# A Mamba block's state scan merged over four channel groups, its input product issued ahead of the product with C, its head in twelve steps, and growing chunks

## The chip, the cores and the metric

The kernel runs on one core of one Trainium2 chip. The metric is the device time of one execution in microseconds (us). The kernel before takes 4009.58 us (median of three runs, 4000.31 to 4012.51). Every run told here was of the fast state, and every kernel's result agreed with the reference. The engines are called PE (TensorE), DVE (VectorE), ACT (ScalarE) and POOL (GpSimd). The account below takes it that each works through its own instructions in the order in which they stand in its queue. The traces agree with that where an engine stands idle in front of one instruction with others behind it; no run tests it. A hole is idle time of an engine between two of its instructions, DVE's where no other is named.

## The reference, cut to what matters

The network has four layers over 3327 nodes. The change lies in layer 1, which runs a graph convolution and puts its normalised output through a Mamba block:

```python
xconv = sum((xpad[k:k + L] * conv_w[:, k] for k in range(D_CONV))) + conv_b
u = jax.nn.silu(xconv)
dbc = u @ w_xp
dt = jax.nn.softplus(dbc[:, :DT_RANK] @ w_dt + b_dt)
B = dbc[:, DT_RANK:DT_RANK + D_STATE]
C = dbc[:, DT_RANK + D_STATE:]
A = -jnp.exp(A_log)
dA = jnp.exp(dt[:, :, None] * A[None])
dBu = dt[:, :, None] * B[:, None, :] * u[:, :, None]

def step(hst, inp):
    dAt, dBut, Ct = inp
    hst = dAt * hst + dBut
    return (hst, hst @ Ct)
_, ys = lax.scan(step, jnp.zeros((D_INNER, D_STATE), h.dtype), (dA, dBu, C))
y = ys + u * D_skip
y = y * jax.nn.silu(z)
return y @ w_out
```

There are 512 inner channels (four groups of 128 partitions) and 16 states. The nodes, padded to 3328, are the sequence. The recurrence runs along it, so channels lie on partitions and nodes on the free axis, in chunks of up to 512.

## The kernel before

For each chunk and each of the 16 states, the kernel does this (cut; `w` is the chunk's width, `NG` is 4, `DS` is 16):

```python
def rows(x, s):                       # issued one state ahead
    parts, dt, du = x
    pb = psum.tile([P, WC], F32, name="ps")[:, :w]
    nc.tensor.matmul(pb, three[:, s:s + 1].to_broadcast([3 * BC, P]), parts, ...)   # B on all partitions
    B = work.tile([P, 1, WC], F32, name="row", bufs=2)[:, :, :w]
    nc.scalar.copy(B[:, 0, :], pb)                                                  # "the row"
    dA = work.tile([P, NG, WC], F32, name="dA")[:, :, :w]                           # two buffers
    for g in range(NG):
        nc.scalar.activation(dA[:, g, :], dt[:, g, :], AF.Exp, scale=A[:, g, s:s + 1])
    return B, dA

def scan(x, s, B, dA):
    C = cpsum.tile([P, 1, WC], F32, name="C")[:, :, :w]
    nc.tensor.matmul(C[:, 0, :], three[:, DS + s:DS + s + 1].to_broadcast([3 * BC, P]), parts, ...)
    db = [...]                                                                      # input product, two halves
    for i in range(2):
        nc.vector.tensor_mul(db[i], du[:, 2 * i:2 * i + 2, :], B.to_broadcast([P, 2, w]))
    h = work.tile([P, NG, WC], F32, name="h")[:, :, :w]
    for g in range(NG):                                                             # four scans
        nc.vector.tensor_tensor_scan(h[:, g, :], dA[:, g, :], db[g // 2][:, g % 2, :],
                                     initial=carry[:, s, g:g + 1], op0=ALU.mult, op1=ALU.add)
    nc.scalar.copy(carry[:, s, :], h[:, :, w - 1])
    nc.vector.tensor_mul(h, h, C.to_broadcast([P, NG, w]))                          # product with C
    return h
```

The row and C are made by PE in PSUM, the memory that PE writes its results to; few PSUM buffers are shared by all these steps. `carry` keeps the last value of each scan, with which the next chunk starts. After each product with C, four matmuls with the identity add `h` to the sums over states (`y` in the profile). Between these stands other work on the same queues. `pump()` does a step of the graph convolution (four matmuls at a time, then its norm and transposes; `rs` in the profile is the norm's factor, a power that GpSimd makes). The states 2 to 5 project the gate. The states 7 to 15 run the head of the next chunk in steps, which makes its `u`, `parts`, `dt` and `du`. `back()` writes out the chunk that ended. The head's costliest step for ACT and PE is this one, called the dt step below:

```python
for g in range(NG):
    ps = psum.tile([P, WC], F32, name="ps")           # two buffers, shared with the row's matmul
    nc.tensor.matmul(ps[:, :w], w_dt[3 * BC:, g * P:(g + 1) * P], left[3 * BC:], ...)
    nc.scalar.activation(v[:, g, :], ps[:, :w], AF.Identity, bias=b_dt[:, g:g + 1])
    nc.scalar.activation(e[:, g, :], ps[:, :w], AF.Abs, bias=b_dt[:, g:g + 1])
```

Of the kernel before, what the change touches and what calls it, by code (L numbers as in the profile page):

```python
# [9 lines left out]
F32 = mybir.dt.float32  # L10
BF16 = mybir.dt.bfloat16
I32 = mybir.dt.int32
AF = mybir.ActivationFunctionType
# [29 lines left out]
def gnn_kernel(ctx: ExitStack, tc: tile.TileContext, n: int, a: dict, out: bass.AP):  # L43
# [88 lines left out]
    with tc.tile_pool(name="l1b", bufs=1) as wpool, tc.tile_pool(name="l1at", bufs=2) as l1at:  # L132
# [29 lines left out]
        with tc.tile_pool(name="l1aw", bufs=1) as cwork, tc.tile_pool(name="l1c", bufs=2) as ch, \  # L162
# [50 lines left out]
            nch = -(-npad // WC)  # L213
            ends = [npad - c * WC for c in range(nch)][::-1]
# [8 lines left out]
            def convolve():  # L223

                rest = None
                for it in range(nt):
                    cb = cpsum.tile([P, 2, D], F32, name="cb")
                    acc, tp = cb[:, 0, :], cb[:, 1, :]
                    for j in range(nt):
# [5 lines left out]
                        if j % JC == JC - 1:  # L235
                            if rest is not None:
                                rest()
                                rest = None
                            yield it
                    m = cwork.tile([P, D], F32, name="m")  # L240
                    nc.scalar.copy(m, acc)
                    yield it
# [9 lines left out]
                    mv = small.tile([P, 2], F32, name="mv")  # L252
                    stats(mv, h)
                    rs = small.tile([P, 1], F32, name="rs")
                    power(rs, mv[:, 1:2])
                    standardize(h, h, mv[:, 0:1], rs)

                    def rest(it=it, h=h):
# [9 lines left out]
                    yield it  # L268
                rest()
                yield nt  # L270
# [42 lines left out]
            def head(c):  # L313
# [7 lines left out]
                nc.vector.tensor_copy(xc[:, :, :3], last)  # L321
                u = us[c] = ch.tile([P, NG, WC], F32, name="u")[:, :, :w]
                for g in range(NG):
                    nc.scalar.copy(xc[:, g, 3:3 + w], project(c, g, w))
                    ug = u[:, g, :]
                    nc.scalar.activation(ug, xc[:, g, 0:w], AF.Identity, scale=conv_w[:, g, 0:1],
                                         bias=conv_b[:, g:g + 1])
                    for k in range(1, 4):
                        nc.vector.scalar_tensor_tensor(ug, xc[:, g, k:k + w], conv_w[:, g, k:k + 1], ug,
                                                       op0=ALU.mult, op1=ALU.add)  # L330
                    yield None
                nc.vector.tensor_copy(last, xc[:, :, w:w + 3])
                nc.scalar.activation(u, u, AF.Silu)
                yield None
# [7 lines left out]
                nc.scalar.copy(left, ps[:3 * BC + DTR, :w])  # L342
                nc.vector.tensor_sub(left[:3 * BC], left[:3 * BC], parts)
                for k in (1, 2):
                    nc.scalar.copy(parts[k * BC:(k + 1) * BC], left[k * BC:(k + 1) * BC])
                nc.vector.tensor_sub(parts[2 * BC:], left[2 * BC:3 * BC], parts[2 * BC:])
# [3 lines left out]
                v, e, e1 = (scratch()[:, :, :w] for _ in range(3))  # L350
# [6 lines left out]
                yield None  # L357
                nc.scalar.activation(e, e, AF.Exp, scale=-1.0)
                nc.scalar.activation(e1, e, AF.Identity, bias=1.0)
                nc.vector.scalar_tensor_tensor(e, e1, 1.0, e, op0=ALU.subtract, op1=ALU.subtract)  # L360
                nc.scalar.activation(e1, e1, AF.Ln)
# [8 lines left out]
                yield parts, dt, du  # L370

            def gate_input(c, g):
                w = us[c].shape[2]
                if g == 0:
                    szs[c] = ch.tile([P, NG, WC], F32, name="sz", bufs=1)[:, :, :w]
                nc.scalar.activation(szs[c][:, g, :], project(c, NG + g, w), AF.Silu)

            def rows(x, s):

                parts, dt, du = x  # L380
# [5 lines left out]
                dA = work.tile([P, NG, WC], F32, name="dA")[:, :, :w]  # L386
                for g in range(NG):
                    nc.scalar.activation(dA[:, g, :], dt[:, g, :], AF.Exp, scale=A[:, g, s:s + 1])  # L388
                return B, dA

            def scan(x, s, B, dA):

                parts, dt, du = x
                w = dt.shape[2]
# [3 lines left out]
                db = [work.tile([P, 2, WC], F32, name="db", bufs=3)[:, :, :w] for _ in range(2)]  # L398
                for i in range(2):
                    nc.vector.tensor_mul(db[i], du[:, 2 * i:2 * i + 2, :], B.to_broadcast([P, 2, w]))  # L400
                h = work.tile([P, NG, WC], F32, name="h")[:, :, :w]
                for g in range(NG):
                    nc.vector.tensor_tensor_scan(h[:, g, :], dA[:, g, :], db[g // 2][:, g % 2, :],  # L403
                                                 initial=carry[:, s, g:g + 1], op0=ALU.mult, op1=ALU.add)
                nc.scalar.copy(carry[:, s, :], h[:, :, w - 1])
                nc.vector.tensor_mul(h, h, C.to_broadcast([P, NG, w]))  # L406
                return h

            def gate(c, ys):
                u = us[c]  # L410
                w = u.shape[2]
                for g in range(NG):
                    nc.vector.tensor_mul(u[:, g, :], ys[g][:, :w], szs[c][:, g, :])

            def back(c):

                u = us[c]
                m = u.shape[2] // P
# [20 lines left out]
            for x in head(0):  # L439
                pump()  # L440
# [730 lines left out]
```

## Time and profile before

| kernel before | us |
|---|---|
| span of the profiled run | 4006.0 |
| first scan starts | 450.3 |
| node 768 done (third 512 chunk opens) | 763.0 |
| last product with C ends | 1677.9 |
| layer 2 entered (its first result) | 1707.7 |
| rest of the program | 2298.3 |

The prediction below shows the views that this was read from. One is added here: the waits of DVE in a single steady chunk (1142 to 1333 us), because the block's totals hide where the time lies. The columns are the engine, what waited, what it waited for, the us in total, the number of waits and the longest.

```profile
DVE h L406 <- PE C L396: 4.9, 2, 3.0
DVE m L87 <- POOL rs L221: 3.7, 4, 1.6
...
DVE db L400 <- ACT row L385: 1.9, 2, 1.0
```

A chunk of 191 us thus has only 15 us of holes, from many releasers. The row of B costs hardly 2 of them.

### The profile page before, as it was taken

To read this page: it belongs to the slowest core of one execution; us is meant where nothing else is said; L and a number is where in the kernel's file an instruction comes from. 1 tells how busy PE (TensorE), PEld (TensorE's weight loads), DVE (VectorE), ACT (ScalarE), POOL (GpSimd) and SP (SyncE) were. 2 spreads that over 40 slices of the span, in tenths; PEclk is the share of its full clock that TensorE was granted. 3 is DMA by queue.
4 is the path that set the end of the run, shared out by engine and by line. 5 is a ranking of instruction groups with operands and counts; after the bars stand their busy time and mean duration, and the time that the engine had idled before them with its cause. 6 is when DMAs were issued, how large, how long until landed. Compare 5 with 4: busy or idle time off the path is not lost.

```text
span 4006.0 us, 41676 instructions
## 1 busy us (share of the span) xinstructions
PE 3596.0 (90%) x15071; PEld 2625.0 (66%) x15071; DVE 2724.7 (68%) x6003; ACT 1675.1 (42%) x2690; POOL 367.1 (9%) x436
## 2 busy tenths in 40 slices
PE   8999988888888877689999999999999899999985
PEld 7888754444444433378877777777777677777764
DVE  1111589999999989867743443443452999999996
ACT  0000555455554555211112333333344666666662
POOL 0000000101010101011110000000000122222210
PEclk9999999999999988889999999999999999999997
DMA  6442211111111000044422111121102122122100
GB/s 218 138 143 92 76 50 40 35 40 35 35 35 37 20 0 0 15 146 142 142 83 75 56 59 49 52 60 57 46 24 86 58 62 62 53 61 61 54 22 7
DMA packets 98960, 252.96 MB, mean 63 GB/s; under 512 B 13858, under 2 KB 48034, under 8 KB 98610
## 3 DMA queue, kind: packets, MB, share of 16 engines
q1 hardware_dynamic: 98738, 250.14, 20.0%
q8 instruction: 122, 2.00, 0.2%
q14 instruction: 100, 0.82, 0.1%
HBM read 239.88 MB, written 10.22 MB: 62 GB/s over the span
## 4 chain that ended last, share of the span: by engine, by line
PE 34%; DVE 16%; ACT 3%; issue 2%; POOL 2%; DMA 0%; POOLq 0%; ACTq 0%; DVEq 0%
PE acc L751 11%; PE acc L719 7%; PE acc L649 6%; PE sc L707 3%; DVE cand L759 3%; DVE e L892 2%; DVE e L893 2%; PE tp L747 2%; PE pj L917 1%; DVE z L829 1%; DVE top L768 1%; DVE z L873 1%; DVE rest L770 1%; ACT junk L827 1%; ACT junk L848 1%
## 5 line engine op out<-in xcount | busy, mean ns | idle before, releaser
L403 DVE TENSOR_TENSOR_SCAN h<-dA,carry,db 128x512 f32<-128x512 f32 (+1 forms) x448 | 510.7, 1191 | 0.1
L459 PE MATMUL y<-h,ident 128*128 128x512 f32 (+1 forms) x896 | 436.1, 633 | 76.7 <-DVE h L406 76.6
L759 DVE MAX8 cand<-e 128x8 f32<-128x128 f32 x676 | 143.8, 280 | 494.6 <-ACT e L708 494.6
L751 PE MATMUL acc<-G,wt 128*128 128x256 f32 x1352 | 342.9, 408 | 48.4 <-ACT wt L749 48.4
L459 PEld LDWEIGHTS y<-h,ident 128*128 128x128 f32 x896 | 185.9, 215 | 290.8 <-issue 175.9
L749 ACT COPY wt<-tp 128x512 f32<-128x512 f32 (+1 forms) x364 | 185.9, 552 | 438.3 <-PE tp L747 438.2
L751 PEld LDWEIGHTS acc<-G,wt 128*128 128x128 f32 x1352 | 268.9, 204 | 120.7 <-ACT wt L749 82.2
L234 PE MATMUL cb<-F,at 128*128 128x256 f32 x1352 | 334.2, 393 | 9.3 <-ACT m L251 9.2
L708 ACT COPY e<-sc 128x416 f32<-128x416 f32 (+1 forms) x416 | 192.5, 508 | 327.8 <-PE sc L707 327.8
L751 PE MATMUL acc<-X,wt 128*128 128x256 f32 x1352 | 326.0, 386 | 3.0 <-ACT wt L749 2.8
L719 PE MATMUL acc<-X,at 128*128 128x256 f32 x1352 | 320.8, 387 | 2.7 <-POOL e L701 2.7
L234 PEld LDWEIGHTS cb<-F,at 128*128 128x128 f32 x1352 | 261.1, 196 | 90.9 <-issue 33.5
L649 PE MATMUL acc<-F,at 128*128 128x257 f32 x1352 | 311.2, 384 | 2.5 <-DVE at L646 2.5
L719 PE MATMUL acc<-F,at 128*128 128x256 f32 x1352 | 308.8, 380 | 0.0
L113 PE MATMUL acc<-xa,at 128*128 128x257 f32 x1352 | 308.3, 381 | 0.0
L719 PEld LDWEIGHTS acc<-X,at 128*128 128x128 f32 x1352 | 250.8, 191 | 76.1 <-issue 41.8
L751 PEld LDWEIGHTS acc<-X,wt 128*128 128x128 f32 x1352 | 250.3, 191 | 63.8 <-ACT wt L749 33.5
L388 ACT ACTIVATE dA<-dt,A_log 128x512 f32<-128x512 f32 (+1 forms) x448 | 280.9, 681 | 12.6 <-DVE dt L365 12.2
L707 PE MATMUL sc<-kT,q 64*128 64x416 f32 x832 | 259.8, 561 | 26.0 <-ACT e L708 26.0
L113 PEld LDWEIGHTS acc<-xa,at 128*128 128x128 f32 x1352 | 255.7, 191 | 37.5 <-issue 0.7
L719 PEld LDWEIGHTS acc<-F,at 128*128 128x128 f32 x1352 | 249.5, 189 | 46.5 <-issue 13.7
L649 PEld LDWEIGHTS acc<-F,at 128*128 128x128 f32 x1352 | 254.1, 192 | 37.4 <-DVE at L646 2.7
(297 smaller groups left out, 5358.7 us busy)
## 6 DMA issues: line engine op xcount, KB each, us to landing
at<-in_adjT SPq DMA_DIRECT2D x104, 832.0 KB, 4.4
at<-in_adjT SPq DMA_DIRECT2D x156, 448.0 KB, 3.3
at<-in_adjT SPq DMA_DIRECT2D x52, 576.0 KB, 3.7
at<-in_adjT SPq DMA_DIRECT2D x52, 320.0 KB, 2.9
at<-in_adjT SPq DMA_DIRECT2D x26, 512.0 KB, 3.5
xa<-in_x SPq DMA_DIRECT2D x1, 3328.0 KB, 13.5
xt<-in_xT SPq DMA_DIRECT2D x26, 128.0 KB, 4.0
qd<-q SPq DMA_DIRECT2D x52, 64.0 KB, 1.5
```

What stands on the lines that cost most here:

```text
L113: nc.tensor.matmul(acc, at[:, j, :], rhs[:, j0 + j, :], start=(j0 + j == 0), stop=(j0 + j == nt - 1))
L234: nc.tensor.matmul(acc, at[:, j % JC, :], X0[:, j, :], start=(j == 0), stop=(j == nt - 1))
L388: nc.scalar.activation(dA[:, g, :], dt[:, g, :], AF.Exp, scale=A[:, g, s:s + 1])
L403: nc.vector.tensor_tensor_scan(h[:, g, :], dA[:, g, :], db[g // 2][:, g % 2, :], initial=carry[:, s, g:g + 1], op0=ALU.mult, op1=ALU.add)
L459: nc.tensor.matmul(ys[g][:, :w], ident, h[:, g, :], start=False, stop=(s == DS - 1))
L649: nc.tensor.matmul(acc, at[:, j, :], F[:, j0 + j, :], start=(j0 + j == 0), stop=(j0 + j == nt - 1))
L707: nc.tensor.matmul(pl[:, :w], q[h:h + DA, :], kT[p][h:h + DA, c0:c0 + w], start=True, stop=True)
L708: nc.scalar.copy(e[:, c:c + w], pl[:, :w])
L719: nc.tensor.matmul(acc, at[:, j, :], rhs[:, j0 + j, :], start=(j0 + j == 0), stop=(j0 + j == nt - 1))
L749: nc.scalar.copy(wt[:, :m, :], pt[:, :m, :])
L751: nc.tensor.matmul(acc, wt[:, j, :], rhs[:, j0 + j, :], start=(j0 + j == 0), stop=(j0 + j == nt - 1))
L759: nc.vector.max(cand[:, s * 8:(s + 1) * 8], z[:, s * SEG:(s + 1) * SEG])
```

## The change

The change means to take instructions and waits off DVE, the full engine, and to start it earlier. It puts a column in front of each group, with decay 0 and the carried state as input, so that one scan runs over all four groups. It issues the next state's input product ahead of the product with C. It moves the carry copies and some small steps to GpSimd, and standardizing to ACT. It spreads the head of the next chunk over twelve states, and it lets the chunks grow: 128, 256, 384, then 512. The core of the diff (the split of the convolution's steps and of the end of a chunk is cut):

```diff
-            nch = -(-npad // WC)
-            ends = [npad - c * WC for c in range(nch)][::-1]
+            ends = []
+            while not ends or ends[-1] < npad:
+                prev = ends[-1] if ends else 0
+                ends.append(min(npad, prev + min(WC, (len(ends) + 1) * P)))
+            nch = len(ends)
...
-                    standardize(h, h, mv[:, 0:1], rs)
+                        nb = small.tile([P, 1], F32, name="nb")
+                        nc.gpsimd.tensor_scalar(nb, mv[:, 0:1], rs, -1.0, op0=ALU.mult, op1=ALU.mult)
+                        nc.scalar.activation(h, h, AF.Identity, scale=rs, bias=nb)
...
-                nc.scalar.activation(szs[c][:, g, :], project(c, NG + g, w), AF.Silu)
+                nc.scalar.copy(szs[c][:, g, :], project(c, NG + g, w))
...
-                dA = work.tile([P, NG, WC], F32, name="dA")[:, :, :w]
+                dA, db = (by_group(x[s % 2], w) for x in (dAs, dbs))
+                if s < 2 and (c == 0 or w != ends[c - 1] - starts[c - 1]):
+                    nc.gpsimd.memset(dA[:, :, 0:1], 0.0)
+                nc.gpsimd.tensor_copy(db[:, :, 0], carry[:, s, :])
...
-                for g in range(NG):
-                    nc.vector.tensor_tensor_scan(h[:, g, :], dA[:, g, :], db[g // 2][:, g % 2, :],
-                                                 initial=carry[:, s, g:g + 1], op0=ALU.mult, op1=ALU.add)
-                nc.scalar.copy(carry[:, s, :], h[:, :, w - 1])
-                nc.vector.tensor_mul(h, h, C.to_broadcast([P, NG, w]))
+                nc.vector.tensor_tensor_scan(h[:, :m], dAs[s % 2][:, :m], dbs[s % 2][:, :m],
+                                             initial=0.0, op0=ALU.mult, op1=ALU.add)
+                nc.gpsimd.tensor_copy(carry[:, s, :], h[:, :, w])
...
+                    if nxt:
+                        B = rows(*nxt)
+                    h = scan(x, s)
+                    if s == 0 and c:
+                        gate(c - 1, ys)
+                    if nxt:
+                        feed(*nxt, B)
+                    nc.vector.tensor_mul(h, h, C.to_broadcast([P, NG, w]))
+                    if nxt:
+                        C = reader(*nxt)
...
-                    if s >= DS - 9 and c + 1 < nch:
+                    if s == 8:
+                        nc.scalar.activation(szs[c], szs[c], AF.Silu)
+                    if DS - 13 <= s < DS - 1 and c + 1 < nch:
```

## The prediction

> **What bounds the kernel now.** I read the busy tenths of the page first, to find the stage that the change touches, then busy time by stretch, then the waits of the vector engine (DVE), then the groups by shape, then the order in time.
>
> The page, the span in 40 slices of 100 us:
>
> ```profile
> PE   8999988888888877689999999999999899999985
> DVE  1111589999999989867743443443452999999996
> ACT  0000555455554555211112333333344666666662
> ```
>
> The Mamba block is the stretch from slice 4 to slice 16: DVE stands at 9 while ACT stands at 5 and TensorE (PE) at 8, and TensorE's busy time has modelled ends, so it is less full than it looks. The graph convolution of the same layer runs inside this stretch on TensorE, and its work there ends near 1397 us.
>
> The stretches are the chunks of the sequence; their borders I took from the products du<-dt,u that open each chunk (441, 575, 763, 954, 1142, 1333, 1520 us) and the last gate (1680 us). After the length come busy us with instruction counts, granted clock, DMA share, GB/s:
>
> ```profile
> core 0: us, PE busy (x) PEld busy (x) DVE busy (x) ACT busy (x) POOL busy (x), PEclk, DMA share, GB/s
> 442.00:575.00 133.00, 118.55 (x511) 88.01 (x510) 101.28 (x146) 81.19 (x166) 3.80 (x8) 1.00 0.21 64
> 575.00:763.00 188.00, 159.19 (x471) 88.30 (x472) 172.04 (x155) 98.30 (x162) 10.87 (x12) 0.93 0.12 37
> 763.00:954.00 191.00, 164.97 (x497) 93.00 (x496) 175.44 (x161) 97.27 (x161) 16.73 (x14) 0.93 0.12 36
> ...
> 1333.00:1520.00 187.00, 143.15 (x371) 70.04 (x370) 173.20 (x155) 103.27 (x188) 13.41 (x10) 0.87 0.01 3
> 1520.00:1680.00 160.00, 115.47 (x287) 55.37 (x286) 155.69 (x129) 75.76 (x158) 11.20 (x6) 0.87 0.00 0
> ```
>
> A chunk of 512 lasts 187 to 191 us, of which DVE works 172 to 176: it is the bound, with about 15 us of holes per chunk. The first chunk (256 wide) is different: 133 us for 101 us of DVE work, with no engine full; it is ruled by handovers. Over 450 to 1690 us DVE is busy 1133 of 1240 us. The view of its waits says what the 107 us of holes are:
>
> ```profile
> DVE h L406 <- PE C L396: 26.2, 13, 3.1
> DVE db L400 <- ACT row L385: 24.9, 16, 6.8
> DVE m L87 <- POOL rs L221: 21.7, 21, 4.0
> ```
>
> The groups by shape, for the cost of one instruction (mean ns after the comma):
>
> ```profile
> L403 DVE TENSOR_TENSOR_SCAN h<-dA,carry,db 128x512 f32<-128x512 f32 x384 | 467.4, 1267 | 0.1
> L400 DVE TENSOR_TENSOR db<-du,row 128x1024 f32<-128x1024 f32 x192 | 229.9, 1213 | 15.1 <-ACT row L385 14.9
> L406 DVE TENSOR_TENSOR h<-h,C 128x2048 f32<-128x2048 f32 x96 | 218.8, 2280 | 23.1 <-PE C L396 20.7 <-ACT carry L405 2.4
> L403 DVE TENSOR_TENSOR_SCAN h<-dA,carry,db 128x256 f32<-128x256 f32 x64 | 43.2, 732 | 0.0
> ```
>
> These means overstate what an instruction occupies, because neighbours overlap. The order in time shows it:
>
> ```profile
> 1658.07 2.28 DVE L406 TENSOR_TENSOR h<-h,C 128x2048 f32<-128x2048 f32 x1
> 1660.27 1.22 DVE L400 TENSOR_TENSOR db<-du,row 128x1024 f32<-128x1024 f32 x1
> 1661.41 4.80 DVE L403 TENSOR_TENSOR_SCAN h<-dA,carry,db 128x512 f32<-128x512 f32 x4
> 1666.13 1.20 DVE L400 TENSOR_TENSOR db<-du,row 128x1024 f32<-128x1024 f32 x1
> 1667.25 2.28 DVE L406 TENSOR_TENSOR h<-h,C 128x2048 f32<-128x2048 f32 x1
> ```
>
> From start to start, four scans take 4.72 us (1.18 each, not 1.267), a half input product 1.12 and the product with C 2.20. One state takes 9.17 us. It also shows that the order on the engine is not the program's: half of the next state's input product already stands between the scans and the product with C.
>
> **What the Trainium skill says.** "VectorE: DVE Perf Modes", section on the TRN2 errata: a fixed extra latency per instruction, so few large tiles are cheaper than many small ones. The trace agrees but makes it small: from 256 to 512 elements the scan's start-to-start time goes from 0.65 us (four in 2.67 us, the last one 0.73) to 1.18, that is 2.08 ns per element and about 0.11 us fixed. "SBUF — State Buffer", section Who interferes with whom: a DVE instruction with two SBUF inputs blocks a GpSimd instruction that reads SBUF until it finishes. The trace agrees: the 128x1 addition on GpSimd at 826.36 took 1.10 us beside a scan that ran 826.19 to 827.44, where alone (379.98) it took 0.22. "ScalarE: Activation LUTs", section What ACT_TABLE_LOAD costs: 1283 ns per switch of set; the trace has exactly that mean.
>
> **The change, part by part.**
>
> One scan for the four groups. A first column per group carries the state (its decay is 0), so the scan has 4 x 513 = 2052 elements: estimated 0.11 + 2052 x 0.00208 = 4.39 us instead of 4.72. The input product becomes one instruction, some 2.20 us (as the product with C) instead of 2.24. A 512 state needs 8.79 us of DVE instead of 9.17: 0.38 us, times 16 is 6.1 us a chunk. From the mean durations it would look like twice that (three scans less at 0.19 us); the overlap has eaten it already.
>
> The new carry copy. It goes from ACT (0.20 us, own port) to GpSimd and reads h, and the product with C overwrites h, so it must wait. The big input product (two SBUF inputs) starts right behind the scan, so GpSimd gets the port only when that ends; the product with C can start about 0.1 us after the end of the input product, where it now starts 0.08 us before the end of its predecessor. I charge 0.18 us a state: 2.9 us per chunk, 23 us for 128 states.
>
> Normalising. The DVE standardize (26 times about 0.36 us occupied) goes to ACT: 1.5 us a chunk, and the wait for GpSimd's rs (21.7 us) falls away. The normalised output goes from GpSimd (8.8 us per chunk beside scans) to ACT, off the path, except some 2 us at the end of the block.
>
> C and B earlier, head in twelve steps. The C matmul is issued directly behind the product with C, so the 26 us should nearly vanish. The row for B keeps much of its wait, I guess 15 of 25 us. The other holes, some 33 us, I leave at 20. Table loads fall too (one Silu for the gate instead of four separate ones), but ACT is only half busy: worth little.
>
> Per 512 chunk with convolution: DVE 175 - 6.1 - 1.5 - 0.3 = 167, holes about 10 (of them 2.9 by GpSimd): 177 us instead of 190. The chunk that comes next to last: 165 + 9 = 174 instead of 187. The last: 149.5 + 5.5 = 155 instead of 160.
>
> Growing chunks 128, 256, 384, then five of 512, instead of 256 and six of 512. The scan starts after one tile of the convolution. Before, the first scan starts at 450.3, 75 us after the first tile's sum; I expect about 420. But the convolution's tiles still have to be paid on TensorE: a matmul in it takes 0.213 us (235 in 50 us at 250 to 300 us), 52 per tile with some transposes: 12.8 us a tile. Summing TensorE's real occupancy (512-wide halves at 0.43 us, 256-wide at 0.21) up to the end of token 768, I get about 281 us for the new order against 290 for the old one, and the old order needs 388 us for it (375 to 763): 75% full. DVE's own work in the new order there is about 275 us, and could not end before 695. I take 80 to 85% fill of TensorE, so token 768 is done near 735 us instead of 763: 28 us. An additional chunk costs fixed parts: 16 states x about 0.5 us, inside that figure.
>
> Sum: 735 + 3 x 177 + 174 + 155 = 1595 us at the last gate instead of 1680: 85 us, and 2 us in the tail. 4010 - 87 = 3923; I say 3925.
>
> **Rivals.** (1) GpSimd's copy costs more than 0.18 us a state: its queue is in order, and the power steps for the norms (0.56 us and up to 2 us, blocked by scans of now 4.4 us) stand in it ahead of carry copies. At 0.5 us a state, 41 us more come back: about 3965. For it: blocked durations of 1.1 us in the trace; against it: only five such norms per chunk, and the input product shields 2.2 us. (2) TensorE becomes the bound. Its real work per 512 chunk, counted as above, is 143.5 us at full clock, at 0.94 some 153; the new chunk of 177 leaves 14%. Lateness of B rows would hold the scan loop, and the time stay near 3960. Against it: the lower clock appears where TensorE idles (0.87 after 1350 us, 1.00 in the full stage before), so a denser queue should run faster. (3) All holes close and the start is DVE-bound: 700 + 3 x 171 + 168 + 151 = 1532, in total near 3860. (4) The fixed parts scale with the mean durations (0.75 us saved per state) and no GpSimd gap: about 3880.
>
> **Range and chances.** The rivals pull to both sides by 40 us, the first three chunks alone by 30. So 3880 to 3975. The 2% line is 3929, almost on my estimate: 0.52 faster, 0.45 same. A slowdown needs both rival 1 and 2 in strong form: 0.03. Nothing after the block is changed, so the rest should keep its length within noise (the runs before spread by 12 us).
>
> **What would show it.** Right: scans of 2052 elements near 4.4 us, start to start of a 512 state near 9.0 us, holes before the product with C of about 0.1 us put down to GpSimd's carry, no wait for rs on DVE, first scan near 420 us, token 768 near 735, chunks of 177. Wrong: gaps over 0.4 us before the product with C (rival 1); input products waiting for the B row with TensorE full (rival 2); a first chunk of 128 longer than 100 us; or an order on DVE where the product with C follows its scan directly.

## The result, and the profile after

The kernel after takes 4041.24 us (median of four runs, 4036.47 to 4044.45), beside 4011.05 us for the kernel before (four runs by then). The ratio is 1.0076, with a 95% interval of 1.0050 to 1.0102. Ratios here and below are the mean time of one kernel's fast runs over that of the other's of the same rounds, so not quite the ratio of the quoted medians. By the 2% rule this is "the same"; in fact it is slightly slower, 66 us above the prediction's upper end.

Where the time came from, from the marks of the two profiled runs (the chunk borders are taken as in the prediction):

| stretch | before | after | difference |
|---|---|---|---|
| up to node 768 done | 763.0 | 766.3 | +3.3 |
| the five 512 chunks, to the last product with C | 915.0 | 942.8 | +27.8 |
| tail, to layer 2's first result | 29.8 | 36.2 | +6.4 |
| rest of the program | 2298.3 | 2295.8 | -2.5 |
| sum (the spans; parts rounded) | 4006.0 | 4041.0 | +35.0 |

The page after, of its 40 slices the rows of DVE and ACT:

```profile
DVE  1111678888888889957744344434452999999997
ACT  0001655544445464311112333333344666666662
```

Counted from 0, DVE stood at 9 in slices 6 to 13 before and stands at 8 there now. It is less full in the block. Busy time by stretch (columns as in the prediction) says that this is not only because it has less to do:

```profile
766.00:968.00 202.00, 171.68 (x507) 98.23 (x508) 168.13 (x89) 94.15 (x150) 32.22 (x53) 0.89 0.11 35
...
1163.00:1360.00 197.00, 160.80 (x486) 91.95 (x486) 167.91 (x92) 94.52 (x150) 40.39 (x50) 0.90 0.10 29
1360.00:1549.00 189.00, 134.19 (x334) 62.85 (x333) 165.72 (x85) 99.68 (x182) 30.75 (x40) 0.84 0.00 0
```

DVE's work in a steady chunk fell from 175 to 168 us, as predicted. But the chunk grew from 191 to 197 us: 29 us of holes in place of 15. The granted clock of PE fell too, from 0.94 to 0.90. The groups by shape, with the mean ns after the comma, confirm the work:

```profile
L431 DVE TENSOR_TENSOR_SCAN h<-dA,db 128x2052 f32<-128x2052 f32 x80 | 353.8, 4424 | 3.1 <-PE y L507 1.5
...
L424 DVE TENSOR_TENSOR db<-du,row 128x2048 f32<-128x2048 f32 x80 | 182.5, 2283 | 66.6 <-ACT row L411 65.7 <-DVE du L385 0.5
```

The scan itself has 3.1 us of idle time in front of it in 80 instances, and the input product has 66.6. In order of time, an input product looks like this at one of its bad places:

```profile
1203.37 2.29 DVE L424 TENSOR_TENSOR db<-du,row 128x2048 f32<-128x2048 f32 x1 [5.66 <-ACT row L411]
1205.58 2.28 DVE L499 TENSOR_TENSOR h<-h,C 128x2048 f32<-128x2048 f32 x1
1207.78 4.42 DVE L431 TENSOR_TENSOR_SCAN h<-dA,db 128x2052 f32<-128x2052 f32 x1
```

The input product stands between scan and product with C, as the change wants, and waits 5.66 us for the row of B. DVE's waits over the block (375 to 1720 us) sum this up:

```profile
DVE db L424 <- ACT row L411: 115.4, 45, 9.1
DVE u L342 <- ACT u L337: 34.0, 10, 12.2
...
DVE h L499 <- POOL carry L434: 20.6, 54, 1.2
...
```

The row wait was 31.7 us over the same stretch before; now it is 115.4. The wait for the norm's rs (25.5 over this stretch) has gone, and the wait for C fell from 26.2 to 6.7. GpSimd's carry costs 20.6 us, where the prediction charged 23.

Why is the row late though ACT works only half the time? ACT's and PE's order in time shows it at two places. The first is in front of a row wait of 5.31 us at 1118.07. ACT first:

```profile
1110.22 0.72 ACT L417 ACTIVATE dA<-dt,A_log 128x512 f32<-128x512 f32 x1 [6.75 <-DVE h L431]
...
1111.73 0.67 ACT L369 ACTIVATE t<-ps,b_dt 128x512 f32<-128x512 f32 x1
...
1116.86 0.70 ACT L370 ACTIVATE t<-ps,b_dt 128x512 f32<-128x512 f32 x1
1117.43 0.60 ACT L411 COPY row<-ps 128x512 f32<-128x512 f32 x1
```

PE in the same stretch:

```profile
1113.98 1.98 PE L367 MATMUL ps<-t,w_dt 16*128 16x512 f32 x4
...
1116.85 0.38 PE L409 MATMUL ps<-parts,three 96*128 96x512 bf16 x1
```

ACT wants to make the decay dA two states ahead, but dA has two buffers and one is still being read. So it stands idle for 6.75 us until the scan ends. Behind this in its queue are the eight reads of the dt step, and PE's last two dt matmuls (the two groups that start at 1113.98) need the PSUM buffers that those reads free. The matmul of the row stands behind them on PE, and the copy of the row behind the reads on ACT. The row is ready 0.6 us after its copy starts, and DVE starts at 1118.07. A wait of ACT for DVE has thus come back as a wait of DVE for ACT.

The second place is the wait of 5.66 us at 1203.37 shown above. Here the first link is GpSimd's power step for the norm of the chunk before, and ACT's normalising waits for it:

```profile
1193.43 5.12 POOL L224 TENSOR_TENSOR rsc<-rsc,mhalf 128x4 f32<-128x4 f32 x1
```

```profile
1199.20 2.07 ACT L472 ACTIVATE X<-X,nbc,rsc 128x256 f32<-128x256 f32 x4 [8.92 <-POOL nbc L468]
```

PE's transposes wait for ACT in turn (7.65 us), and the row's matmul at 1202.08 and its copy at 1202.76 come after both.

One small loss is separate from all this, the tail. The load of layer 3's weight W is issued at a different point. The DMA queue in order of time, before:

```profile
1690.32 0.33 SPq L67 DMA_DIRECT2D W<-in_W  x1
```

and after:

```profile
1736.83 0.33 SPq L67 DMA_DIRECT2D W<-in_W  x1
```

Before, it waited for the matmuls with w_out, some 16 us ahead of the block's last work. After, it waits for the last of the block's value steps on PE and ACT, so that load and matmuls of W follow the block instead of lying beside it. The queue shows this; no run tests it. The variants of the kernel after that follow all have a tail of 33.2 to 36.8 us, and those of the kernel before 29.5 to 31.9.

### The profile page after: what moved, and what is told of

The parts are those of the page before. It is cut to its first block, busy times and chain, and to the rows that moved or that the text cites. A ratio compares the mean times of both kernels' runs of the same rounds, so it can differ in the third digit from the quotient of the medians.

```text
span 4041.0 us, 42245 instructions
## 1 busy us (share of the span) xinstructions
PE 3597.1 (89%) x15287; PEld 2655.8 (66%) x15287; DVE 2678.6 (66%) x5585; ACT 1672.9 (41%) x2714; POOL 497.2 (12%) x734
## 4 chain that ended last, share of the span: by engine, by line
PE 51%; DVE 30%; ACT 7%; issue 5%; POOL 5%; DMA 1%; SPq 0%; ACTq 0%; POOLq 0%; DVEq 0%
PE acc L804 11%; PE acc L772 7%; PE acc L113 7%; DVE h L431 7%; PE acc L702 7%; PE sc L760 3%; PE y L507 3%; DVE db L424 3%; DVE cand L812 3%; DVE h L499 3%; PE cb L238 2%; DVE e L945 2%; DVE e L946 2%; PE tp L800 2%; ACT dA L417 2%
## 5 line engine op out<-in xcount | busy, mean ns | idle before, releaser
L431 DVE TENSOR_TENSOR_SCAN h<-dA,db 128x2052 f32<-128x2052 f32 (+3 forms) x128 | 463.8, 3624 | 6.1 <-ACT dA L417 1.6
L507 PE MATMUL y<-h,ident 128*128 128x512 f32 (+3 forms) x1024 | 446.5, 579 | 3.2 <-DVE h L499 3.2
L417 ACT ACTIVATE dA<-dt,A_log 128x512 f32<-128x512 f32 (+3 forms) x512 | 293.8, 634 | 302.6 <-DVE h L431 272.7
L507 PEld LDWEIGHTS y<-h,ident 128*128 128x128 f32 x1024 | 209.7, 217 | 295.8 <-issue 270.5
L424 DVE TENSOR_TENSOR db<-du,row 128x2048 f32<-128x2048 f32 (+3 forms) x128 | 241.0, 1884 | 116.5 <-ACT row L411 115.4
L772 PEld LDWEIGHTS acc<-F,at 128*128 128x128 f32 x1352 | 249.5, 189 | 46.4 <-issue 13.7
```

The lines of the kernel that those rows point to most:

```text
L417: nc.scalar.activation(dA[:, g, 1:], dt[:, g, :], AF.Exp, scale=A[:, g, s:s + 1])
L424: nc.vector.tensor_mul(by_group(dbs[s % 2], w)[:, :, 1:], du, B.to_broadcast([P, NG, w]))
L431: nc.vector.tensor_tensor_scan(h[:, :m], dAs[s % 2][:, :m], dbs[s % 2][:, :m], initial=0.0, op0=ALU.mult, op1=ALU.add)
L507: nc.tensor.matmul(ys[g][:, :w], ident, h[:, g, :], start=False, stop=(s == DS - 1))
L772: nc.tensor.matmul(acc, at[:, j, :], rhs[:, j0 + j, :], start=(j0 + j == 0), stop=(j0 + j == nt - 1))
```

## The experiments

Times are medians, and ratios are against the kernel before of the same rounds (its medians there: 4009.24, 4007.47, 4005.34, 4005.93 and 4005.24 us for the five groups of runs). All used three rounds. Everything said below of a trace is of the profiled run of that kernel. Differences in us are differences of medians. The kernel before had medians from 4005.24 to 4011.05 us in the different rounds, so across groups a difference is good to some 6 us (the 72 us of the early row below are 66 by the ratios). Where two intervals of the ratio overlap, I call two kernels not told apart.

**The parts of the change, one at a time.** The first eight runs each undo one part in the kernel after, or put one part into the kernel before.

*The one scan, cut into four.*

```diff
-                nc.vector.tensor_tensor_scan(h[:, :m], dAs[s % 2][:, :m], dbs[s % 2][:, :m], initial=0.0, ...)
+                for g in range(0, m, 1 + w):
+                    nc.vector.tensor_tensor_scan(h[:, g:g + 1 + w], dAs[s % 2][:, g:g + 1 + w], dbs[s % 2][:, g:g + 1 + w], initial=0.0, ...)
```

> The changed kernel with the one scan of 2052 elements cut into four of 513 (same buffers, same order), nothing else. Port theory (a 4.4 us scan with two SBUF inputs holds GpSimd's reads; GpSimd's power steps for the norms come late, ACT and TensorE stand behind them in order, and the row for B reaches the vector engine late): the power step at the start of a chunk, now 5.12 us, falls under 2.5 us, the waits of the input product for the row fall from 115 us to about 75, while the scans take 128 x 0.34 = 43 us more; the time stays near 4041 (4020 to 4055). Order theory (the waits come from the input product being placed directly behind the scan, whatever the scan's length): the waits stay at 105 to 125 us, the time goes to about 4080.

Measured: 4019.74 us, ratio 1.0026 (1.0018 to 1.0035), 21 us faster than the kernel after although it has more instructions and more work. The row wait fell from 115.4 to 97.4 us. The order theory fell. Of the port theory the power step came true (on four values its mean over five chunks fell from 3.49 to 1.57 us), while the row wait fell by less than half of what it said. This run also corrects a size of the prediction. From start to start, a scan of 513 elements with the constant 0 as its initial value takes 1118 ns; the old scan of 512 elements with its initial value per partition took 1177 ns; the merged one takes 4343 ns. So of the 4.71 - 4.34 = 0.37 us per state that the change saves, 4 x 0.059 = 0.24 come before any merging, and only 4 x 1.118 - 4.343 = 0.13 come from merging. The first part most likely comes from the constant initial value, which the extra column makes possible; the layout of the tiles differs too, and no run separates the two.

*The norm's standardizing back on DVE.*

```diff
-                        nb = small.tile([P, 1], F32, name="nb")
-                        nc.gpsimd.tensor_scalar(nb, mv[:, 0:1], rs, -1.0, op0=ALU.mult, op1=ALU.mult)
-                        nc.scalar.activation(h, h, AF.Identity, scale=rs, bias=nb)
+                        standardize(h, h, mv[:, 0:1], rs)
```

> The changed kernel with the convolution's norm applied on the vector engine as before (GpSimd still makes the power), instead of nb on GpSimd and the normalising on ACT. Port theory: ACT no longer stands waiting for nb (90.8 us now) and TensorE's transposes no longer for that (38.6 us); of the row waits the 5.6 us ones at the start of each chunk shrink, in all from 115 to about 85 us; the vector engine gets 9 us of work and some 15 us of waits for rs back: 4025 to 4040. Order theory: row waits stay over 105 us, and the added work and waits make it 4055 to 4070.

Measured: 4022.07 us, ratio 1.0029 (1.0019 to 1.0039), 19 us faster than after and 3 us under the port theory's range. Row waits fell to 83.8 us, close to its 85; a wait of 24.9 us for GpSimd's rs came back. Taking a task off the bounding engine and putting it on ACT's queue, behind GpSimd, did not pay.

*The product with C first again.*

```diff
-                    if nxt:
-                        feed(*nxt, B)
                     nc.vector.tensor_mul(h, h, C.to_broadcast([P, NG, w]))
+                    if nxt:
+                        feed(*nxt, B)
```

> The changed kernel with the product with C issued before the next state's input product. Order theory: the row has 2.2 us more before it is needed; waits for it fall from 115 us to 50 or less (the part of each wait under 2.2 us sums to 66 us), the product with C now waits openly for GpSimd's carry copy, about 0.3 us x 128 = 38 us instead of 21: 4000 to 4020. Port theory: the row's lateness is set by GpSimd's chain and moves along; waits stay over 90 us, the time 4035 to 4060.

Measured: 4037.76 us, ratio 1.0072 (1.0055 to 1.0089), within the noise of after. The row wait is 120.7 us: the order theory, which said 50 or less, fell. The new order gives and takes nothing here, although it needs the row 2.2 us earlier.

*The old chunks (256, then six of 512) in the kernel after.*

```diff
-            ends = []
-            while not ends or ends[-1] < npad:
-                ...
+            nch = -(-npad // WC)
+            ends = [npad - c * WC for c in range(nch)][::-1]
```

> The changed kernel with the chunks of before (256 and six of 512) instead of 128, 256, 384 and five of 512. If the growing chunks are neutral (token 768 was done at 766 us after and 763 before): within 8 us of the changed kernel, 4033 to 4049. If the small chunks cost (53 of the 115 us of row waits lie in the first three chunks, and there are 16 states more): 4010 to 4030. If they gain what was meant (the first scan at 417 instead of 450): 4060 to 4075.

Measured: 4032.26 us, ratio 1.0056 (1.0039 to 1.0073), 9 us under after, just under the range for neutral chunks, and not told apart from the kernel after. The first scan starts at 439.2 us instead of 417.5, and yet node 768 is done at 762.9 instead of 766.3. The earlier start brings nothing in this kernel.

*The merged scan alone, in the kernel before* (carry on ACT as before; one buffer of `u`, with the gate written into `sz`, to make room; the merged scan's first column also takes one more small copy on ACT per state, in front of the decays).

```diff
-                for g in range(NG):
-                    nc.vector.tensor_tensor_scan(h[:, g, :], dA[:, g, :], db[g // 2][:, g % 2, :],
-                                                 initial=carry[:, s, g:g + 1], ...)
+                nc.vector.tensor_tensor_scan(h[:, :m], dAs[s % 2][:, :m], dbs[s % 2][:, :m], initial=0.0, ...)
```

> The kernel before with the one scan of 2052 elements alone (state column, decay 0; carry copies on ACT; two half input products as before; u in one buffer and the gate written to sz, for room). If the long scan hurts only through what the change put on GpSimd and behind it (norm chain, carry copies, normalising on ACT): the vector engine saves about 112 x 0.34 = 38 us, GpSimd's power steps make the standardize wait longer (21.7 us to about 45): 3985 to 4005. If the long scan itself is the loss, by holding GpSimd's port whatever the rest: 4020 to 4045.

Measured: 4041.93 us, ratio 1.0091 (1.0075 to 1.0108), 34 us slower than the kernel before. Its row wait is 78.6 us (31.7 before), and its wait for rs is 43.0 (25.5). So the merged scan, with these edits that it needs, costs as much as the whole change. How much of the 34 us is the copy or the single buffer, no run shows.

*The growing chunks alone, in the kernel before* (with the steps of the convolution at the start spread as in the change).

```diff
+            while not ends or ends[-1] < npad:
+                prev = ends[-1] if ends else 0
+                ends.append(min(npad, prev + min(WC, (len(ends) + 1) * P)))
```

> The kernel before with the growing chunks alone (and the pumps of the start that go with them). Chunks neutral or slightly costly, as old chunks in the changed kernel gave 9 us back: 4008 to 4025. Chunks a gain that the changed kernel lost elsewhere: 3975 to 3995.

Measured: 3998.58 us, ratio 0.9975 (0.9967 to 0.9982), 9 us faster than the kernel before, between the two ranges. Here the first scan starts at 406.8 us. Node 768 is no earlier than before, at 766.5; the gain shows in the chunks that follow, 185 to 188 us each for the four before the last.

*The carry's copy back on ACT.*

```diff
-                nc.gpsimd.tensor_copy(carry[:, s, :], h[:, :, w])
+                nc.scalar.copy(carry[:, s, :], h[:, :, w])
```

> The changed kernel with the copy of the carry from h on ACT again instead of GpSimd. Port theory: the product with C no longer waits for GpSimd (20.6 us), and the norm chain has GpSimd more to itself: row waits fall from 115 to about 90 us; 4005 to 4025. Order theory (queues of ACT and TensorE decide, not GpSimd): ACT takes one more wait for the scan into its queue, the rows come no earlier: 4030 to 4050.

Measured: 4018.94 us, ratio 1.0032 (1.0018 to 1.0046), 22 us faster than after, in the port theory's range. The wait for the carry grew to 38.5 us, now for ACT; the row wait fell from 115.4 to 85.9.

*The gate's projections late, in states 11 to 14 instead of 2 to 5*, with the Silu in state 15 and a third buffer for the convolution's output.

```diff
-                    if 2 <= s < 2 + NG:
-                        gate_input(c, s - 2)
-                    if s == 8:
+                    if DS - 1 - NG <= s < DS - 1:
+                        gate_input(c, s - (DS - 1 - NG))
+                    if s == DS - 1:
```

> The changed kernel with the gate's four projections moved from states 2 to 5 (where the head's projections of the next chunk now fall too, states 3 to 6) to states 11 to 14, and its Silu to state 15; hT gets a third buffer for that. Crowding theory (the head in twelve steps starts four states earlier and shares the two PSUM buffers and ACT with the gate): row waits in states 3 to 7 (about 25 us) and the waits for u on ACT (34 us, 12 of them in the start) fall by 25 us together: 4010 to 4025. Port theory: it changes little, 4033 to 4048.

Measured: 4004.85 us, ratio 0.9998 (0.9989 to 1.0007), 36 us faster than after (31 by the ratios), better than both theories said. In the change, gate and head projections fall into the same states 3 to 5, share the PSUM buffers there, and are both read by ACT. Still the row wait is 112.5 us: what fell is the wait for u (34.0 to 15.9). That is 18 us; where the rest of the gain comes from was not traced.

So no part of the change stands alone as the culprit: four different edits give 19 to 36 us each. Three of them change what stands in the queues of ACT and GpSimd, the fourth (four scans) how long both wait for DVE.

**Do these gains add up?** The next runs join late gates with other edits.

*Late gates and four scans* (both edits above).

> The after kernel with the gate projections in late states (as e8) and the one scan cut into four again. Granularity theory (a scan of 4.4 us that nothing can break into delays every small VectorE and GpSimd step behind it, and late gates only took away one of the collisions): both gains are partly separate, 3980 to 3998 us, waits of the input product for the B row below 90 us. Rival (fixed queues only move the idle time about; e1 and e8 removed the same idle time): within 8 us of e8, 3997 to 4013 us.

Measured: 4007.53 us, ratio 1.0008 (0.9999 to 1.0017). The rival was right: no better than late gates alone.

*Late gates and the carry on ACT.*

> The after kernel with late gates and the carry's copy on ScalarE in place of GpSimd. Theory (the copies on GpSimd stand in the way of its norm steps and of the scan; worth 22 us alone): 3983 to 3998 us, with the VectorE waits for GpSimd's carry (20.6 us) gone and about half of them back as waits for ScalarE. Rival: same as e8 within 8 us.

Measured: 3994.89 us, ratio 0.9973 (0.9961 to 0.9985). The time lies in the theory's range, 10 us under late gates alone: less than half of the carry's 22 us.

*Late gates and the dt step split in two.*

```diff
                     nc.scalar.activation(e[:, g, :], ps[:, :w], AF.Abs, bias=b_dt[:, g:g + 1])
-                yield None
-                nc.vector.tensor_sub(parts[2 * BC:], left[2 * BC:3 * BC], parts[2 * BC:])
+                    if g == 1:
+                        yield None
+                        nc.vector.tensor_sub(parts[2 * BC:], left[2 * BC:3 * BC], parts[2 * BC:])
```

> The after kernel with late gates and the head step of the dt projection split in two (groups 0 and 1 in its own state, groups 2 and 3 with the exponential's step). Theory (on TensorE the product with C for the scan stands behind four groups of dt matmuls and ScalarE behind four reads of them, which makes the row of B late by 5 to 9 us once a chunk): the longest wait of each chunk falls to 1 to 4 us, 3965 to 3988 us. Rival (the wait is set by the scan, not by this step): within 8 us of e8.

Measured: 3997.06 us, ratio 0.9973 (0.9963 to 0.9982), 8 us under late gates alone, at the edge of the rival's range. The longest row wait fell from 8.9 to 5.6 us, not to the 1 to 4 expected.

*All four edits, one scan kept* (late gates, split dt step, carry on ACT, standardizing on DVE).

> The after kernel with the one scan kept, and four other edits at once: late gates, split dt step, carry on ScalarE, norm's standardizing on VectorE. Theory (one scan is worth its 43 us once nothing small waits behind it): 3940 to 3975 us, below the kernel before by over 0.8%. Rival (idle time only moves): 3990 to 4010 us.

Measured: 4005.97 us, ratio 0.9997 (0.9988 to 1.0006): the rival. The row wait did fall, to 54.7 us, but waits for rs (23.8) and for the convolution's output (25.5, of which 11.6 stand before the first scan, as in the kernel after) took its place.

*The same without the edit of the norm.*

> The run with all edits at once without its norm edit (late gates, split dt step, carry on ScalarE; standardizing on ScalarE again). Theory (VectorE standardizing costs its 1.7 us of work a chunk plus waits for GpSimd's rs, 24 us there): 3975 to 3992 us. Rival (the three edits remove the same waits twice, norm is not to blame): 4000 to 4010 us.

Measured: 4013.68 us, ratio 1.0017 (1.0009 to 1.0024). This missed both ranges: taking the norm's edit away made it 8 us slower, so in this combination the norm is not to blame. The split dt step gains 8 us without the carry on ACT, and with it the time is 19 us longer (4013.68 against 3994.89). Which two places collide in this case stays open. Edits that each shorten one wait do not add up.

**The row earlier in the queue.** If the lateness is one of place in a queue, then moving the row itself should be worth more than clearing things from its way. Its buffer of two already allows it: the row of state s was last read one state before the row of s+2 is written.

```diff
                 for g in range(NG):
                     nc.scalar.activation(dA[:, g, 1:], dt[:, g, :], AF.Exp, scale=A[:, g, s:s + 1])
+                if s + 1 < DS:
+                    early[s + 1] = row(s + 1)     # the matmul and copy of the row, now two states ahead of use
                 return B
```

(Cut: the helper `row` around the old matmul and copy, and the line that takes the row from `early`.)

> The after kernel with one edit: the matmul and the copy that make the B row of a state are issued one state earlier (two states ahead of their use), in front of all the other TensorE and ScalarE work of that state. Theory (the one scan itself is worth its time, and is eaten because the row comes late: 115 us of waits): waits of the input product for the row fall to 20 to 50 us, chunks of 512 to 178 to 186 us, time 3960 to 4000 us. Rival (idle time is set by the total of the fixed queues, a wait taken away comes back elsewhere, on the carry, the decay or C): 4015 to 4045 us, with the waits of DVE for the decay or for C grown.

Measured: 3968.88 us, ratio 0.9912 (0.9896 to 0.9929). One edit makes the kernel after 72 us faster, and faster than the kernel before. The theory's range of the time held. Its range of the row wait did not: 61.2 us are left. Over the block the row wait fell by 54 us, while the wait for C rose from 6.7 to 32.4. DVE's waits in the steady chunk 1163 to 1360 us of the kernel after are these:

```profile
DVE db L424 <- ACT row L411: 14.4, 5, 5.7
DVE u L342 <- ACT u L337: 4.2, 1, 4.2
DVE h L499 <- PE C L442: 3.0, 1, 3.0
...
```

and in the same chunk with the early row (1122 to 1309 us):

```profile
DVE db L433 <- ACT row L415: 12.3, 2, 9.4
DVE h L508 <- PE C L451: 2.0, 2, 1.2
...
DVE u L342 <- ACT u L337: 1.6, 2, 1.3
```

The row waits are fewer (2 instead of 5), but one is longer. Of the 9 us of holes that this chunk lost, only 2.1 are row wait; the waits for u (2.6), for the parts of the head (2.6), for the carry (2.0) and for C (1.0) fell as well, and one new wait of 1.7 us came. So "the row is late" was the largest symptom, and not the only one, of queues that are late. In three chunks the long wait of 9.37 us is at state 13, where the row still stands behind the dt step. There PE, too, waited 5.74 us, and the matmuls after that wait were slow: two y matmuls took 2.08 us at 1081.43, where two took 1.02 us at 1063.43, and the granted clock was 0.50 from 1078 to 1088 us. This agrees with the Trainium skill, "TensorE: Matmul & The Clock Gate", Part 1 on the HAM clock gate: after an idle window of about 3.4 us PE runs at half its clock until it has been busy for a while. A long wait of PE is thus followed by slower work of PE, with the next row in it (its matmul at 1087.30 took 0.63 us, that at 1062.99 0.38); how much of the loss this makes was not measured.

*The early row in the kernel before* (the same edit in its `rows`).

> The kernel before with the same edit (its row waits are 31.7 us). Theory: it gains little, 3990 to 4008 us, as its rows were late in few places; then the change's other parts would show their worth as the difference to the after kernel with the early row. Rival (early rows help both alike): 3960 to 3985 us.

Measured: 4046.04 us, ratio 1.0097 (1.0081 to 1.0114), 40 us slower than the kernel before. Neither range held. The row wait fell from 31.7 to 19.7 us, but other waits rose: for GpSimd's rs from 25.5 to 38.6, for ACT in the head's exponential step from 1.1 to 32.1, and a wait of the scan for the y matmuls of 33.3 us appeared that is not in the list of before. An early row is thus no gain in itself. It seems to push other things back in a queue that was in balance; this is read from the waits, and no run tests it.

*The early row, with late gates, split dt step and carry on ACT.*

> Early row together with late gates, split dt step and carry on ScalarE, one scan kept. Theory: row waits below 30 us, chunks near 178 us, 3940 to 3975 us, below both kernels. Rival: no better than the best of the single edits, 3985 to 4005 us.

Measured: 3982.72 us, ratio 0.9940 (0.9923 to 0.9957): between the two ranges, and 14 us slower than the early row alone. Again, gains do not add.

*The early row and the split dt step.*

> The early row with the dt projection's step split in two. In the run with the early row, the row of state 13 was late by 9.37 us in three chunks, behind four groups of dt matmuls on TensorE. Theory: that wait falls below 4 us in each chunk, some 25 us over the block, time 3938 to 3955 us, over 1.2% below the kernel before. Rival (the split's second half delays the exponential's step instead, as in the run with all edits): 3965 to 3985 us.

Measured: 3949.76 us, ratio 0.9856 (0.9825 to 0.9887). The theory held. In the three steady chunks the wait at state 13 fell from 9.37 to 1.82 us. This kernel is 1.4% faster than the kernel before.

*The early row and four scans.*

> The early row with the one scan cut into four again. With the late row, cutting it made the kernel 21 us faster. Theory (the one scan is worth its 0.35 us a state, some 40 us, once the row is early): slower than with one scan, 3990 to 4012 us. Rival (a scan of 4.4 us is harmful in itself, to small instructions of VectorE and to GpSimd, early row or not): 3945 to 3970 us.

Measured: 3952.54 us, ratio 0.9867 (0.9845 to 0.9890). The rival was right, and my theory of the merged scan fell: with the row early, four scans are still 16 us faster than one. The stretches of a steady chunk, with one scan:

```profile
1122.00:1309.00 187.00, 161.23 (x496) 91.09 (x496) 166.65 (x91) 95.06 (x150) 30.91 (x50) 0.92 0.10 31
```

and with four:

```profile
1106.00:1286.00 180.00, 158.47 (x497) 91.49 (x496) 168.63 (x139) 95.66 (x148) 25.62 (x50) 0.93 0.12 35
```

Four scans cost DVE 2.0 us more work per chunk, and save 9 us of holes (20.4 to 11.4). ACT's waits between 760 and 1640 us, again with one scan and then with four:

```profile
ACT dA L424 <- DVE h L440: 221.2, 62, 8.7
```

```profile
ACT dA L424 <- DVE h L441: 180.4, 151, 7.5
```

Four scans give the buffer of dA back in quarters, 1.12 us apart, so ACT waits in more and shorter pieces, and by my estimate starts on them up to 3.3 us sooner (three scans of 1.12). At state 13, the row wait in the three steady chunks is 3.9 to 4.3 us instead of 9.4. A single scan gives everything back at its end. That this early release is the cause is argued from the trace; a long scan also keeps DVE's own small steps (sums, statistics) waiting up to 4.3 us and blocks GpSimd for as long, and no run tells these three apart. In the kernel before, ACT copies the carry after the end of all four scans and makes the decays behind that, so there early release to ACT can't explain why merging cost time.

Two of these kernels beat both kernels by 1.3 to 1.4%: the early row with the split dt step, and the early row with four scans. Their intervals overlap. All three edits together were not run.

## Why the prediction was wrong

| step of the prediction | predicted | measured |
|---|---|---|
| first scan | 420 us | 417.5 us |
| merged scan, start to start | 4.39 us | 4.34 us |
| a 512 state without row wait or other work of DVE | near 9.0 us | mostly 8.9 to 9.3 us |
| DVE work per 512 chunk with convolution | 167 us | 167 to 168 us |
| GpSimd's carry | 23 us | 20.6 us |
| wait for rs, wait for C | gone, nearly gone | gone, 6.7 us |
| wait for the row, 450 to 1690 us | 15 us | 108.2 us |
| other holes (not rs, C, carry), 450 to 1690 us | 20 us | 52 us |
| holes per 512 chunk | 10 us | 28 to 34 us |
| node 768 done | 735 us | 766.3 us |
| last gate starts | 1595 us | 1711.2 us |
| tail | -2 us | +6.4 us |

The cost of each instruction was right; what failed is the step "Per 512 chunk with convolution: DVE 175 - 6.1 - 1.5 - 0.3 = 167, holes about 10". I took the holes as a stock from which the change removes its waits and keeps the rest. The runs showed that they are what is left where one queue waits for another. DVE needed 8 us less in a chunk, as predicted, but the queues of ACT and PE, reordered by the change and with waits for the longer scan and for GpSimd's norm in them, came later. That step cost 85 of the 116 us at the last gate (944.9 against 3 x 177 + 174 + 155 = 860), and "The row for B keeps much of its wait, I guess 15 of 25 us" is the term in it that was wrong by 93 us; "The other holes, some 33 us, I leave at 20" was wrong by 32. Both were guesses, and no line of the trace carried them. That the place of the row in the queues matters is shown by one edit: the early row cut its wait by 54 us and the time by 72. Why the row became so late is shown only in parts that do not add up.

The remaining 31 us come from "token 768 is done near 735 us". The occupancy of PE was taken as the limit, at a fill of 80 to 85%. The sum is wrong there: 281 us at that fill, from 375 us on, end at 706 to 726 us; 735 is a fill of 78%, and 766 is one of 72%. What held the small chunks up was in part the row: between 414 and 766 us DVE waited 49.7 us for it. Node 768 came at 766 us in the kernel after and at 766.5 us with growing chunks in the kernel before, at 755 us once the row was early, and at 748 us with four scans besides. By the profile PE was busy 282 of the 316 us from 450 to 766; its ends are modelled, so a share of PE's own load is not excluded. The prediction had itself found that the first chunk of the kernel before "is ruled by handovers", and did not carry this over.

"One scan for the four groups" was right in its size (0.33 us predicted, 0.37 measured) and wrong in its reason. The fixed cost of 0.11 us per scan was put down to the instruction. The four scans of 513 elements show that most of the saving comes without merging (most likely from the constant initial value), and that merging alone saves 0.13 us a state, 2.1 us a chunk. That is less than what a scan of 4.3 us costs the queues around it: the merged scan cost time in the kernel before (34 us, with the edits that it needed there), in the kernel after (21 us) and with the early row (16 us), and only with late gates made no difference.

"Table loads fall too (...), but ACT is only half busy: worth little" and "Normalising ... goes to ACT" share one fault. They price ACT by its busy share. ACT's idle time is not free when it stands in a wait at the head of an in-order queue with the row behind it.

Rival 2 named the sign, "Lateness of B rows would hold the scan loop", but with a full PE as its cause. PE's busy time in a steady chunk was 161 of 197 us after, where it was 163 of 191 before: PE was not fuller. The argument against it, "a denser queue should run faster", did not come to the test: the queue got less dense, and the granted clock fell from 0.94 to 0.90. Rival 1 charged GpSimd's copy for up to 41 us more at the product with C. That gap came out as predicted. The copy nevertheless costs 22 us more on GpSimd than on ACT, and what fell when it was moved was the row wait.

The tail's -2 us rested on the normalised output moving to ACT. The load of W, issued 12 us after the last product with C before and 28 us after it now, was not looked at.

What stays open: which of early release, small steps and GpSimd's blocking makes the merged scan costly; why the row became late in the kernel after, beyond the two places shown; why the split dt step loses with the carry on ACT; and why the early row hurts the kernel before.

## What to carry to other kernels

A pipeline over in-order queues has no stock of holes that can be subtracted from. If the bounding engine gets faster, read from the trace for each of its inputs how much earlier that input could come, and what stands in front of it in its own queue. Then issue the late one sooner, before merging or moving anything. A merged instruction gives its buffers back later and keeps small steps waiting longer. Here a gain of 0.13 us per merge was lost in three of four comparisons; which of the two lost it is not shown.

## What the Trainium skill lacked or had wrong

- "VectorE: DVE Perf Modes", section on the TRN2 errata, says that many small tiles pay a fixed latency each and advises tiles of 512 elements or more. Here scans of 513 elements were merged to 2052: the fixed cost that this removes is 0.13 us per state, and the merged form made three kernels 16 to 34 us slower (one of them with other edits beside it). The page doesn't mention that a longer instruction gives buffers back later.
- No page I looked up gives the cost of an initial value per partition in a scan: 512 elements with it took 1177 ns from start to start, 513 elements with the constant 0 took 1118 ns.
- "SBUF — State Buffer", section Who interferes with whom, says that a DVE instruction with two SBUF inputs contends with a GpSimd instruction that reads SBUF, and the runs agree: the power step on four values took 5.12 us beside a scan that started 0.15 us before it, and 1.04 us alone. It doesn't say what this means in a queue: ACT's norm step behind it waited 8.93 us for GpSimd, and the row behind that was 5.66 us late.
